# A two-layer decoder on one core: rotary turning by DMA exchange, paired causal tiles, 17-column values and second buffers in layer 1

## The chip, the cores and the metric

The kernel runs on one core of one Trainium2 chip. The metric is device time in microseconds (us) of one execution; the figure for a version is the median of its runs.

## The reference, cut to what matters

The model has two decoder layers over x of 4 sequences x 512 positions x 256 features (16 heads of 16), with a context of 1601 rows per sequence. The change lies in the self-attention of layer 1 and in what it shares with the cross-attention of layer 1:

```python
q = (x @ wq_w + wq_b).reshape(b, l, NH, HD)          # k and v in the same way
# apply_rope, for q and k: first and second are the halves (8 + 8) of a head
out = concatenate([first * cos - second * sin, second * cos + first * sin], -1)
scores = einsum('bnqh,bnkh->bnqk', q, k) / sqrt(HD)
scores = where(causal, scores, lowest)
attn = softmax(scores, axis=-1)
ctx = einsum('bnqk,bnkh->bnqh', attn, v)             # then @ wo_w + wo_b
```

Cross-attention of layer 1 has the same form without turning and mask, over the 1601 context rows. All of it is computed in float32.

## The kernel before, in words

The program has three parts, run one after the other: `front` (layer 0 attentions), `experts` (layer 0 feed-forward) and `heads` (all of layer 1). Only `heads` and the constants that it reads are changed.

`heads` takes the self-attention of all four sequences (`cross` False) and then the cross-attention of all four. A sequence has four groups of four heads (`head_group`, L1060). Two groups share one projection (`projections`, L1024) of 128 features on 128 partitions, called a half here, and one tile of values (`values`, L982).

A self-attention half goes this way. TensorE projects q into a PSUM bank, ScalarE (or VectorE) adds the bias into `q0` (L978). `rope` (L1012) then has TensorE multiply `q0` by a constant 128 x 128 matrix `rot`, which exchanges the halves of each head with a sign (L1014, through the helper at L239, "one<-q,consts" in the profile). VectorE multiplies that bank by the sines into `rt` (L1015), GpSimd multiplies `q0` by the cosines (L1017) and adds both into `qu` (L1019). k takes the same way into `ku`. `apart` (L1069) lets SyncE (SP) issue four DMAs for q and four for k in each group (L1072), which put each head's 16 rows at partition 32j of `qT` and `kT`, so that TensorE can hold four heads in four row lanes of 32.

A group then has two passes. In the first, 16 score units (one head, one block of 128 queries kq; 128, 256, 384 or 512 keys) each take a PSUM bank, "one<-kT,qT", and VectorE takes the largest masked score of each query (L1113). The negated maxima are turned by TensorE (L1147, "one<-consts,nm") and added to `qT`, giving `qa` (L1151), which frees the `qT` slot. In the second pass each of four key tiles t and four heads gives transposed scores, "one<-qa,kT", of 512, 384, 256 or 128 queries; ScalarE takes the exponential (L1173) into one of ten `pe` buffers, GpSimd zeroes the triangle (L1179), and TensorE multiplies four heads' weights by the values in four column lanes, "acc<-pe,v" (L1188). A head's values fill 32 columns: 16 values, a one (it gives the softmax's sum), 15 zeros. ScalarE copies the result (L243), TensorE turns it back (L1208), VectorE divides (L1212, L1220), and `finish` (L1281) projects and normalizes.

The order is made by `Plan` (L54) at build time: every step is a node with an engine, a cost and a priority; the plan keeps model clocks per engine, and issues in order of model start. TensorE nodes have a mode ("row" for four row lanes, "col" for column lanes, "full"), and the plan prefers to stay in one mode for a while. Pools of slots bound it: seven banks `one`, one bank `acc`, two slots of `qT`, `qa`, `v` and `q0`, three of `kT`, one of `rt`, `qu` and `ku`. On the chip each engine runs its list in this order and waits on semaphores[...].

Of the kernel before, what the change touches and what calls it, by code (L numbers as in the profile page):

```python
# [7 lines left out]
F32 = mybir.dt.float32  # L8
# [8 lines left out]
P = 128  # L17
# [12 lines left out]
NS = 31  # L30
NF = 24
# [5 lines left out]
C_ID, C_ROT, C_TRI, C_MQK = 0, 128, 256, 384  # L37
C_COS, C_SIN, C_IE, C_IT, C_IP = 896, 1408, 1920, 1936, 1968
NCONST = 1969
# [141 lines left out]
def cost_mm(n):  # L181

    return n * 4 / 2400
# [19 lines left out]
def tile_decoder(ctx: ExitStack, tc: tile.TileContext, a, out):  # L203
# [697 lines left out]
    def heads():  # L901
        plan = Plan()
        with tc.tile_pool(name="h1", bufs=1) as h1, \
# [5 lines left out]
            def slots(name, n, shape):  # L909
                plan.pool(name, n)  # L910
                return [h1.tile(shape, F32, tag=f"{name}{i}", name=f"{name}{i}") for i in range(n)]
# [4 lines left out]
            VV = slots("v", 2, [P, NKT, H // 2, 32])  # L916
# [9 lines left out]
            Q0, RT = slots("q0", 2, [P, L]), slots("rt", 1, [P, L])  # L926
            QU, KU = slots("qu", 1, [P, L]), slots("ku", 1, [P, LC])

            plan.pool("f", 6)
            FF = [*Q0, *RT, junk, *(h1.tile([P, L], F32, tag=f"f{i}", name=f"f{i}") for i in range(2))]  # L930
# [3 lines left out]
            rot = consts[:, C_ROT : C_ROT + P]  # L934
# [7 lines left out]
            def ones_behind(n, t):  # L942
                nc.gpsimd.memset(t[:, :, :, HD:], 0.0)
                nc.gpsimd.memset(t[:, :, :, HD : HD + 1], 1.0)

            def key_rows(n, k):
                nc.sync.dma_start(KT[k], a["keys0"])

            cleared = N("pool", 1.5, -1.5, clear)
            keyed = [N("dma", 2.5, -4.0, None, [N("sp", 0.4, -4.0, lambda n, k=k: key_rows(n, k))]) for k in range(3)]  # L950
            framed = [N("pool", 5.0, -1.5 + k, lambda n, k=k: ones_behind(n, VV[k])) for k in range(2)]


# [58 lines left out]
            def rope(pr, src, q0, rt, dst, DST):  # L1012

                r = N("pe", cost_mm(L), pr, lambda n: mm(ONE[n.slot], rot, Q0[q0.slot]), [src], take=["one"])  # L1014
                t = N("dve", dve(L), pr, lambda n: nc.vector.tensor_tensor(  # L1015
                    RT[rt.slot], ONE[r.slot], sinT, ALU.mult), [r], free=[r])
                d = N("pool", pool(L), pr, lambda n: nc.gpsimd.tensor_tensor(  # L1017
                    DST[dst.slot][:, :L], Q0[q0.slot], cosT, ALU.mult), [src], free=[q0])
                e = N("pool", pool(L), pr, lambda n: nc.gpsimd.tensor_tensor(  # L1019
                    DST[dst.slot][:, :L], DST[dst.slot][:, :L], RT[rt.slot], ALU.add), [d, t], free=[rt])  # L1020
                plan.frees(r, [q0])
                return e
# [37 lines left out]
            def head_group(cross, b, g, pos, vals, pair, after):  # L1060
# [8 lines left out]
                def apart(DST, dst, SRC, src, n):  # L1069
                    h0 = 64 * (g % 2)  # L1070
                    for j in range(4):
                        nc.sync.dma_start(DST[dst.slot][32 * j : 32 * j + HD, :n],  # L1072
                                          SRC[src.slot][h0 + HD * j : h0 + HD * (j + 1), :n])

                q, k = hold("qT", pr, after), hold("kT", pr, after)
                qd = N("sp", 1.6, pr, lambda n: apart(QT, q, QU, qu, L), [q, cleared, *qs])
                qready = N("dma", 0.5, pr, None, [qd], free=[qu])
                kd = N("sp", 1.6, pr, lambda n: apart(KT, k, KU, ku, nk), [k, *keyed, *ks])
# [6 lines left out]
                if cross:  # L1085
                    for n_ in range(12):
                        kq, m = divmod(n_, 3)
                        units += [(j, m, [(kq, m * 512, m * 512 + 512)]) for j in range(4)]
                else:
                    for kq in range(4):  # L1090
                        units += [(j, 0, [(kq, 0, (kq + 1) * P)]) for j in range(4)]
                maxes, scored = [], []
                for i, (j, m, prods) in enumerate(units):
                    pu = pos - 1.2 + (i + 0.5) / len(units)
                    js = slice(32 * j, 32 * j + 32)
                    nn, w = len(prods), prods[0][2] - prods[0][1]

                    def score(n, prods=prods, js=js, w=w):
                        for i, (kq, k0, k1) in enumerate(prods):
                            mm(ONE[n.slot][:, i * w : (i + 1) * w], QT[q.slot][js, kq * P : (kq + 1) * P],  # L1100
                               KT[k.slot][js, k0:k1])

                    s = N("pe", cost_mm(nn * w), pu, score, [mx], take=["one"], lanes=(j,), mode="row")

                    def largest(n, s=s, j=j, m=m, prods=prods, w=w):
                        nn, kq = len(prods), prods[0][0]
                        t = ONE[s.slot][:, : nn * w]
                        if cross:
                            nc.vector.tensor_reduce(  # L1109
                                MX[mx.slot][:, kq : kq + nn, j, m : m + 1], t.rearrange("p (a n) -> p a n", a=nn),  # L1110
                                AX.X, ALU.max)
                        else:
                            nc.vector.tensor_tensor_reduce(  # L1113
                                out=junk[:, :w], in0=t, in1=m_qk[:, 384 - kq * P : 512],
                                scale=1.0, scalar=NEG, op0=ALU.add, op1=ALU.max,
                                accum_out=MX[mx.slot][:, kq, j, 0:1])

                    maxes.append(N("dve", dve(nn * w), pu, largest, [s], free=[s]))
                    scored.append(s)
# [38 lines left out]
                for t in range(nkt):  # L1158
                    kn = kt_size(t) if cross else P
                    q0 = 0 if cross else t * P  # L1160
                    exps = []
                    for i, j in enumerate((2, 3, 0, 1)):
                        pu = pos + (t + 0.25 * i) / nkt
                        js = slice(32 * j, 32 * j + 32)
                        w = hold("pe", pu, [acc])

                        def score(n, t=t, kn=kn, q0=q0, js=js):
                            mm(ONE[n.slot][:kn, q0:], KT[k.slot][js, t * P : t * P + kn], QA[qa.slot][js, q0:])

                        s = N("pe", cost_mm(L - q0), pu, score, [w, o, *kready], take=["one"], lanes=(j,), mode="row")  # L1170

                        def weigh(n, s=s, w=w, kn=kn, q0=q0):
                            nc.scalar.activation(PE_[w.slot][:kn, q0:], ONE[s.slot][:kn, q0:], AF.Exp, scale=HD**-0.5)  # L1173

                        r = N("act", act(L - q0), pu, weigh, [s], free=[s])
                        if not cross:
                            def causal(n, w=w, q0=q0):
                                d = PE_[w.slot][:, q0 : q0 + P]
                                nc.gpsimd.affine_select(  # L1179
                                    d, d, pattern=[[1, P]], compare_op=ALU.is_ge, fill=0.0,  # L1180
                                    base=0, channel_multiplier=-1)

                            r = N("pool", pool(128), pu, causal, [r])
                        exps.append((w, r))

                    def product(n, t=t, kn=kn, q0=q0, exps=exps):
                        for j in range(4):
                            nc.tensor.matmul(  # L1188
                                ACC[acc.slot][32 * j : 32 * j + 32, q0:],
                                VV[v.slot][:kn, t, 4 * (g % 2) + j, :],  # L1190
                                PE_[exps[j ^ 2][0].slot][:kn, q0:],
                                start=t == 0, stop=t == nkt - 1,
                            )

                    pr_ = last[-1:] if last else []
                    last.append(N("pe", cost_mm(L - q0) + 0.05, pos + (t + 1.2) / nkt, product,
                                  [r for _, r in exps] + vready + pr_, free=[w for w, _ in exps], mode="col"))
# [220 lines left out]
def _constants():  # L1418
# [6 lines left out]
    for j in range(8):  # L1425
        for d in range(8):
            c[16 * j + d + 8, C_ROT + 16 * j + d] = -1.0
            c[16 * j + d, C_ROT + 16 * j + d + 8] = 1.0
# [4 lines left out]
    for d in range(P):  # L1433
        c[d, C_COS : C_COS + L] = np.cos(angle[d % 8])
        c[d, C_SIN : C_SIN + L] = np.sin(angle[d % 8])
# [6 lines left out]
def _layout(i):  # L1442
# [29 lines left out]
    o["w_shared_down"] = T(i["L0_ffn_w_down"])  # L1472
    for n in "qk":
        o[f"w{n}1"] = i[f"L1_attn_w{n}_w"]
        o[f"w{n}2"] = i[f"L1_xattn_W{n}"]
# [9 lines left out]
    cols = [i["L0_xattn_bq"], i["L0_xattn_bk"], i["L1_attn_wq_b"], i["L1_attn_wk_b"],  # L1485
# [29 lines left out]
```

## Time and profile before

| what | value |
|---|---|
| runs, us | 1762.3, 1764.39, 1764.44 |
| median of the runs | 1764.39 us |
| the profiled execution's own time | 1755.73 us |
| its span, first to last instruction | 1754.0 us |
| mean granted TensorE clock in it | 0.967 |
| first and last score unit of layer 1 ("one<-kT,qT") | 540.6 and 1677.8 us |
| last causal triangle (L1179) | 869.2 us |
| busy, 540 to 830 us | TensorE 280.7, VectorE 207.4, GpSimd 119.9, ScalarE 116.9 us |

A row of the groups names line, engine, operation, out<-in, and shapes; then count, busy time in us and mean ns of one. A float32 matmul shows as two records, so "x8" in the timeline is four heads of one matmul each. The timeline has start, duration and the records merged into the piece; a bracket gives the idle time ahead of it and what ended it. Matmul ends are modelled and overlap the next one's start, so lengths are taken from start to start. Self-attention and the first cross-attention group overlap between about 826 and 869 us.

### The profile page before, as it was taken

How to read it: one execution, taken by the hardware profiler on the slowest of the kernel's cores; microseconds unless marked ns; L12 is line 12 of the kernel's file. 1: busy time of each engine (PE TensorE's matmuls, PEld its weight loads, DVE VectorE, ACT ScalarE, POOL GpSimd, SP SyncE). 2: the span in 40 equal slices, each digit the busy share in tenths (PEclk: the TensorE clock that was granted, in tenths of full speed). 3: DMA queues.
4: the chain of work that ended last, by engine and by line, in shares of the span. 5: the costliest groups of instructions: out<-in, count | busy, mean ns of one | idle time of the engine just before them, and what ended most of it. 6: DMA issues, size and time to landing. Idle time of an engine off the chain costs nothing.

```text
span 1754.0 us, 28495 instructions
## 1 busy us (share of the span) xinstructions
PE 1661.4 (95%) x10756; PEld 862.5 (49%) x10756; DVE 1110.2 (63%) x2678; ACT 761.5 (43%) x1593; POOL 342.3 (20%) x521
## 2 busy tenths in 40 slices
PE   7899988999968999999999999999999999999995
PEld 4677775887754444454433334433334333343323
DVE  6997654121237766667776666777667776677625
ACT  0335551211112334444355555456554555545581
POOL 6652003432134534442100000100001000010000
PEclk9999987999988989999999999999999999999998
DMA  9000006876431100001100000001000010001000
GB/s 304 29 4 10 13 26 220 290 238 207 144 108 37 32 10 16 13 19 21 24 1 13 14 14 13 1 13 26 13 14 1 13 26 13 14 1 25 1 1 12
DMA packets 40843, 87.50 MB, mean 50 GB/s; under 512 B 7808, under 2 KB 26752, under 8 KB 37632
## 3 DMA queue, kind: packets, MB, share of 16 engines
q1 hardware_dynamic: 31728, 42.58, 9.0%
q0 software_dynamic: 8832, 43.00, 7.1%
q8 instruction: 86, 1.41, 0.3%
q14 instruction: 53, 0.43, 0.1%
q10 hardware_dynamic: 144, 0.07, 0.0%
HBM read 64.52 MB, written 8.26 MB: 41 GB/s over the span
## 4 chain that ended last, share of the span: by engine, by line
PE 83%; DVE 11%; DMA 2%; issue 2%; ACT 1%; POOL 1%; DVEq 0%; POOLq 0%; SPq 0%; ACTq 0%
PE one L239 53%; PE acc L1188 14%; PE e_one L239 11%; DVE junk L1113 1%; PE one L563 1%; PE one L1147 1%; PE one L1208 1%; DMA xs<-x_dram,tok 1%; PE one L1270 1%; DMA y<-ys_dram,dest 1%; DVE sc L423 1%; DVE pm L528 0%; ACT pe L1173 0%; DVE pr L462 0%; DVE qk L406 0%
## 5 line engine op out<-in xcount | busy, mean ns | idle before, releaser
L1173 ACT ACTIVATE pe<-one 128x512 f32<-128x512 f32 (+4 forms) x1088 | 533.0, 566 | 385.9 <-PE one L239 382.1
L1109 DVE TENSOR_REDUCE mx<-one 128x1 f32<-128x512 f32 x768 | 487.7, 683 | 182.1 <-PE one L239 178.3
L239 PE MATMUL one<-qa,kT 32*128 32x512 f32 (+4 forms) x2176 | 512.6, 600 | 7.7 <-ACT pe L1173 6.3
L239 PE MATMUL one<-kT,qT 32*128 32x512 f32 (+4 forms) x2560 | 500.7, 536 | 8.0 <-DVE mx L1113 2.6
L239 PEld LDWEIGHTS one<-qa,kT 32*128 32x128 f32 (+1 forms) x2176 | 171.8, 182 | 227.8 <-issue 78.0
L1188 PE MATMUL acc<-pe,v 128*32 128x512 f32 (+4 forms) x2176 | 270.7, 569 | 0.0
L239 PEld LDWEIGHTS one<-kT,qT 32*128 32x128 f32 x2560 | 191.5, 185 | 153.8 <-ACT pe L1173 45.3
L1276 POOL TENSOR_TENSOR x<-x,rows 128x1024 f32<-128x1024 f32 x12 | 28.3, 2356 | 802.4 <-PE one L1270 802.4
L1113 DVE CUSTOM_DVE_ANT_0 junk<-one,consts 128x256 f32<-128x256 f32 (+3 forms) x256 | 125.4, 490 | 50.7 <-PE one L239 25.8
L1188 PEld LDWEIGHTS acc<-pe,v 128*32 128x32 f32 (+1 forms) x2176 | 43.9, 108 | 178.6 <-issue 161.9
L1179 POOL TENSOR_SCALAR_AFFINE_SELECT pe<-pe 128x128 f32<-128x128 f32 x256 | 72.5, 298 | 140.9 <-ACT pe L1173 137.3
L239 PEld LDWEIGHTS e_one<-xsT,wgu 128*128 128x128 f32 x768 | 90.7, 194 | 4.8 <-issue 3.8
L239 PE MATMUL e_one<-xsT,wgu 128*128 128x128 f32 x768 | 90.6, 277 | 0.0
L239 PE MATMUL e_one<-xT,w_sgu 128*128 128x512 f32 x128 | 61.8, 624 | 3.1 <-DMA w_sgu<-in_w_shared_gu 3.1
L239 PE MATMUL one<-w_in,xT 128*128 128x512 f32 (+1 forms) x128 | 49.5, 543 | 10.4 <-DMA xT<-in_xT 10.4
L243 ACT COPY o<-acc 128x512 f32<-128x512 f32 x32 | 18.7, 586 | 75.5 <-PE acc L1188 75.5
L239 PE MATMUL one<-ctxT,q 128*128 128x512 f32 (+1 forms) x128 | 49.5, 518 | 0.0
L544 ACT ACTIVATE pe<-one,nm 128x512 f32<-128x512 f32 x64 | 37.3, 596 | 27.8 <-DVE nm L536 27.7
L239 PE MATMUL one<-pT,ctxN 128*128 128x128 f32 (+1 forms) x416 | 49.0, 275 | 0.0
L239 PEld LDWEIGHTS one<-pT,ctxN 128*128 128x128 f32 (+1 forms) x416 | 48.2, 192 | 1.6 <-issue 1.2
L852 DVE TENSOR_TENSOR he<-sg,e_one 128x512 f32<-128x512 f32 x24 | 16.5, 686 | 50.7 <-PE e_one L239 48.1
L830 DVE TENSOR_SCALAR xs<-xs,scs 128x256 f32<-128x256 f32 x24 | 8.5, 364 | 60.3 <-DMA xs<-x_dram,tok 60.3
(261 smaller groups left out, 1866.2 us busy)
## 6 DMA issues: line engine op xcount, KB each, us to landing
kT<-ku SPq DMA_DIRECT2D x64, 100.1 KB, 3.4
qT<-qu SPq DMA_DIRECT2D x128, 32.0 KB, 1.9
ctxN<-in_ctxN SPq DMA_DIRECT2D x4, 832.0 KB, 8.9
ctxT<-in_ctxT SPq DMA_DIRECT2D x4, 800.5 KB, 9.5
ys_dram<-ye SPq DMA_DIRECT2D x24, 128.0 KB, 2.4
kT<-in_keys SPq DMA_DIRECT2D x3, 800.5 KB, 9.7
xT<-in_xT SPq DMA_DIRECT2D x16, 128.0 KB, 3.6
x<-in_x SPq DMA_DIRECT2D x16, 128.0 KB, 6.0
```

The lines of the kernel that those rows point to most:

```text
L239: nc.tensor.matmul(out, lhsT, rhs, start=c == 0, stop=c == n - 1)
L243: nc.scalar.copy(dst, src)
L423: scores.append(N("dve", 1.21, pos + 0.22 + 0.05 * s, lambda n, s=s, pr=pr: nc.vector.tensor_reduce(SC[sc.slot][:, s].rearrange("p t h -> ...
L544: nc.scalar.activation(PE_[w.slot][:, : k1 - k0], ONE[b.slot][:, : k1 - k0], AF.Exp, bias=NM[nm.slot][:, 1:2], accum_out=PS[sm_.slot][:, i ...
L563: nc.tensor.transpose(ONE[n.slot][:kn, (t % 4) * P : (t % 4 + 1) * P], PE_[w.slot][:, (t % 4) * P : (t % 4) * P + kn], ident)
L1109: nc.vector.tensor_reduce(MX[mx.slot][:, kq : kq + nn, j, m : m + 1], t.rearrange("p (a n) -> p a n", a=nn), AX.X, ALU.max)
L1113: nc.vector.tensor_tensor_reduce(out=junk[:, :w], in0=t, in1=m_qk[:, 384 - kq * P : 512], scale=1.0, scalar=NEG, op0=ALU.add, op1=ALU.max, ...
L1147: nc.tensor.transpose(ONE[n.slot][:, kq * P : (kq + 1) * P], NM[nm.slot][:, kq].rearrange("p j r -> p (j r)"), ident)
L1173: nc.scalar.activation(PE_[w.slot][:kn, q0:], ONE[s.slot][:kn, q0:], AF.Exp, scale=HD**-0.5)
L1179: nc.gpsimd.affine_select(d, d, pattern=[[1, P]], compare_op=ALU.is_ge, fill=0.0, base=0, channel_multiplier=-1)
L1188: nc.tensor.matmul(ACC[acc.slot][32 * j : 32 * j + 32, q0:], VV[v.slot][:kn, t, 4 * (g % 2) + j, :], PE_[exps[j ^ 2][0].slot][:kn, q0:], s ...
L1276: rw = N("pool", pool(1024), pos, lambda n: nc.gpsimd.tensor_tensor(XB[b], XB[b], rows[:, row : row + D].unsqueeze(1).to_broadcast([P, 4, ...
```

## The change

1. Turning. The rows of wq and wk (and their biases) are laid out so that the 64 first halves of a half's eight heads lie on partitions 0 to 63 and the second halves on 64 to 127. `rope` no longer multiplies by `rot`: two DMAs exchange the two blocks of 64 partitions of `q0` into `rt`, and the multiplication by the (now signed) sines is given to VectorE or GpSimd. `apart` issues eight DMAs of 8 rows where it issued four of 16, for q and for k.
2. Pairs of masked tiles. The score units of the first pass are (kq 3), (kq 0 and 2), (kq 1), of 512, 128 + 384 and 256 columns; those of the second (t 0), (t 1 and 3), (t 2), of 512, 384 + 128 and 256. A pair shares one bank, and in the second pass one exponential. Maxima stay one instruction for each kq.
3. Values of 17 columns. The 15 zero columns go; `acc` is set to zero once at the start.
4. Second buffers for `rt`, `qu` and `ku`; the tree's pool `f` uses the second `rt` in place of one buffer of its own.

```diff
+MQ = (3,), (0, 2), (1,)
+TQ = (0,), (1, 3), (2,)
...
-            VV = slots("v", 2, [P, NKT, H // 2, 32])
+            VV = slots("v", 2, [P, NKT, H // 2, HD + 1])
...
-            Q0, RT = slots("q0", 2, [P, L]), slots("rt", 1, [P, L])
-            QU, KU = slots("qu", 1, [P, L]), slots("ku", 1, [P, LC])
+            Q0, RT = slots("q0", 2, [P, L]), slots("rt", 2, [P, L])
+            QU, KU = slots("qu", 2, [P, L]), slots("ku", 2, [P, LC])
...
-                r = N("pe", cost_mm(L), pr, lambda n: mm(ONE[n.slot], rot, Q0[q0.slot]), [src], take=["one"])
-                t = N("dve", dve(L), pr, lambda n: nc.vector.tensor_tensor(
-                    RT[rt.slot], ONE[r.slot], sinT, ALU.mult), [r], free=[r])
+                def swap(n):
+                    for i in range(2):
+                        nc.sync.dma_start(RT[rt.slot][64 * i : 64 * i + 64], Q0[q0.slot][64 - 64 * i : 128 - 64 * i])
+
+                r = N("dma", 0.7, pr, None, [N("sp", 0.8, pr, swap, [src])], free=[q0])
+                t = N("dve|pool", (dve(L) + 0.6, pool(L)), pr, lambda n: (nc.vector if n.on == "dve" else nc.gpsimd).tensor_tensor(
+                    RT[rt.slot], RT[rt.slot], sinT, ALU.mult), [r])
...
                     for j in range(4):
-                        nc.sync.dma_start(DST[dst.slot][32 * j : 32 * j + HD, :n],
-                                          SRC[src.slot][h0 + HD * j : h0 + HD * (j + 1), :n])
+                        for i in range(1 if cross else 2):
+                            w = HD if cross else HD // 2
+                            r = (h0 + j) * w + 64 * i
+                            nc.sync.dma_start(DST[dst.slot][32 * j + w * i : 32 * j + w * i + w, :n],
+                                              SRC[src.slot][r : r + w, :n])
...
-                qd = N("sp", 1.6, pr, lambda n: apart(QT, q, QU, qu, L), [q, cleared, *qs])
+                qd = N("sp", 1.6 if cross else 3.2, pr, lambda n: apart(QT, q, QU, qu, L), [q, cleared, *qs])
...
-                    for kq in range(4):
-                        units += [(j, 0, [(kq, 0, (kq + 1) * P)]) for j in range(4)]
+                    for kqs in MQ:
+                        units += [(j, 0, [(kq, 0, (kq + 1) * P) for kq in kqs]) for j in range(4)]
...
+                        def score(n, at=at, js=js):
+                            for t, kn, q0, w in at:
+                                mm(ONE[n.slot][:kn, w : w + L - q0], KT[k.slot][js, t * P : t * P + kn], QA[qa.slot][js, q0:])
+
+                        s = N("pe", cost_mm(w), pu, score, [e, o, *kready], take=["one"], lanes=(j,), mode="row")
+
+                        def weigh(n, s=s, e=e, kn=at[0][1], w=w):
+                            nc.scalar.activation(PE_[e.slot][:kn, :w], ONE[s.slot][:kn, :w], AF.Exp, scale=HD**-0.5)
...
-                                ACC[acc.slot][32 * j : 32 * j + 32, q0:],
+                                    ACC[acc.slot][32 * j : 32 * j + HD + 1, q0:],
```

## The prediction

> **What bounds the kernel now.** I read the page first: TensorE (PE) is busy for 95% of the span and carries 83% of the chain that ended last.
>
> ```profile
> PE 1661.4 (95%) x10756; PEld 862.5 (49%) x10756; DVE 1110.2 (63%) x2678; ACT 761.5 (43%) x1593; POOL 342.3 (20%) x521
> PE 83%; DVE 11%; DMA 2%; issue 2%; ACT 1%; POOL 1%; DVEq 0%; POOLq 0%; SPq 0%; ACTq 0%
> ```
>
> Then the busy times by stage (columns: PE, PEld, DVE, ACT, POOL busy, granted clock, DMA share, GB/s). In the self stage (540 to 830) PE is all but full, VectorE at 71%, the others at 40%; the cross stage is fuller still. So PE's own list is to be counted.
>
> ```profile
> 540.00:830.00 290.00, 280.67 (x1887) 140.09 (x1888) 207.35 (x742) 116.91 (x289) 119.92 (x274) 0.94 0.08 19
> 830.00:1700.00 870.00, 862.38 (x6022) 330.55 (x6020) 606.67 (x1175) 473.90 (x909) 33.77 (x77) 1.00 0.07 12
> ```
>
> What a piece of PE work costs I read from the timeline, start to start, at full clock:
>
> ```profile
> 705.27 1.06 PE L1188 MATMUL acc<-pe,v 128*32 128x512 f32 x8
> 706.26 0.71 PE L239 MATMUL one<-kT,qT 32*128 32x128 f32 x8
> 706.91 0.85 PE L1188 MATMUL acc<-pe,v 128*32 128x384 f32 x8
> 707.69 1.12 PE L239 MATMUL one<-q,consts 128*128 128x512 f32 x2
> 708.74 0.70 PE L239 MATMUL one<-qa,kT 32*128 32x256 f32 x8
> ```
>
> ```profile
> 1111.30 1.06 PE L1188 MATMUL acc<-pe,v 128*32 128x512 f32 x8
> 1112.29 1.14 PE L239 MATMUL one<-kT,qT 32*128 32x512 f32 x8
> 1113.37 1.06 PE L1188 MATMUL acc<-pe,v 128*32 128x512 f32 x8
> ```
>
> Column-lane products of 512 columns take 0.99, of 384 take 0.78: 0.21 for 128 columns (1.64 ns a column), hence 0.84 for 512 and **0.15 left over for each run in that mode**. A row run of 512 takes 1.08 (0.24 left over), one rotation 1.05 (0.21). A row run of four 128-column scores takes 0.65 for 0.21 of columns. So PE's time is columns of the fullest lane x 1.64 ns, plus 0.15 to 0.24 for each change of mode.
>
> **Removed from PE.** I counted both builds' instruction order in layer 1, taking for each run of one mode the lane with most columns. Rotations: 16 x 512 columns go, 16 x 0.84 = 13.4 us. Row lanes: 286,272 becomes 282,688 (the pairs come as four equal lanes more often), 3,584 x 1.64 ns = 5.9 us. Runs: row 404 to 378, full 184 to 165, col 267 to 253: 26 x 0.24 + 19 x 0.21 + 14 x 0.15 = 12.3 us. Together 31.6 us. Four of the rotations run between 525 and 558 us, where PE waits for norms and rotations anyway (busy 33 of 40 us from 520 to 560): 4 x 1.05 = 4.2 us that buy nothing. I take **27.4 us**, about 3.4 us of it in the cross stage (1,536 lane columns, 2.5 us, and five runs).
>
> **Off the path.** ScalarE: four exponentials of 600, 515, 403 and 288 ns become three of 600, 600 and 403, 0.2 x 64 = 13 us less on an engine at 40%; worth nothing while PE has other lanes to issue. VectorE: maxima unchanged (0.69 + 0.08 for 512 columns); 12 of 16 sine products of 0.69 leave it for GpSimd, which takes 12 x 1.27 = 15 us more (the row of the cosine product) and rises from 41 to some 51%. Both hidden by PE. One memset of `acc`, and 3 us less of memset on GpSimd, lie ahead of the first scores. The second `qu` and `ku` add nothing to PE; their worth is the earlier projections in the counted order.
>
> **Values of 17 columns.** No row shows 17. Weight loads take 109 ns for 32 columns and 184 for 128, 0.78 ns a column, so 15 columns fewer save 12 ns a load. If every load were exposed in its lane, 2176 x 12 ns / 4 = 6.5 us; if all are hidden, 0. A loss is not excluded by any row either, but a narrower copy writes the same 64 values per partition, and PE streams the same columns, so I bound it by 1 us. The loads mostly run beside matmuls: I take 0.
>
> **Added: waits on SP.** SP's list and landing times:
>
> ```profile
> 599.72 2.41 SPq L1072 DMA_DIRECT2D kT<-ku  x4
> 602.42 2.40 SPq L1072 DMA_DIRECT2D qT<-qu  x4
> ```
>
> ```profile
> qT<-qu SPq DMA_DIRECT2D x68, 32.0 KB, 1.9
> ```
>
> An issue costs 0.58 us (2.41 / 4 is 0.60), a landing 1.9. Now q needs eight: 8 x 0.58 + 1.9 = 6.5 us from `qa` (which frees the `qT` slot) to the last lane of the group after next, where it was 4.2. Each lane waits only for its own two DMAs, so lane 0 is ready after 3.1. Behind `qa` PE has in its list the 12 second-pass units of that group, a projection (1.9) and products (1.0), 5 us or more. The last lane can be late by 0 to 2 us in 14 groups, 0 to 28 us in all; most groups have cover, so I take 0.3 each, 4 us. SP's total is (256 + 64) x 0.58 = 186 us of some 265, and not a bound.
>
> **The exchange.** Bias to sine product was one matmul (1.05); now two issues and a landing, 1.2 + 1.9 = 3.1 us. 128 KB each could take longer: DMAs of 100 KB land in 3.5, so 3 to 5 us. SP issues the exchange of the next half behind eight q DMAs that wait for `qa`. If it is late, GpSimd stands in front of the sine product, and the triangles behind it on GpSimd hold the products on PE. The second `rt`, `qu` and `ku` let it start about a group (16 us) ahead. Between 0 and 2.5 us for each of six later halves: I take 2 us in all, near the low end since before, GpSimd held the weight loads of the products for 5.2 us in all this stage. At the start, q and k reach `qT` one exchange later, but two matmuls and VectorE's queue earlier: even. I take 0 of -4 to +4.
>
> The Trainium skill ("SBUF — State Buffer", its rule on the shared port pair) says that VectorE's two-input operation with both inputs in SBUF excludes a GpSimd operation that reads SBUF, for the whole instruction. The sine product was PSUM by SBUF, and becomes such a case. Row: GpSimd's cosine product is 1.27 us, VectorE's sine product 0.69. By the row alone nothing is added; by the rule four products left on VectorE block or are blocked once each, at most 4 x 1.3 = 5 us. No trace here shows a lock; I take 0 and keep 5 for the range.
>
> A second rule speaks against the change: "TensorE: Matmul & The Clock Gate", on the clock gate, has PE fall to half clock after some 3.4 us without work. This trace shows the price:
>
> ```profile
> 615.00 2.34 PE L239 MATMUL one<-kT,qT 32*128 32x512 f32 x4 [2.56 <-DVE mx L1113]
> ```
>
> ```profile
> 600.00:620.00 20.00, 17.44 (x110) 7.51 (x102) 15.78 (x55) 7.41 (x20) 12.82 (x23) 0.90 0.18 47
> 620.00:640.00 20.00, 20.00 (x130) 9.61 (x129) 10.45 (x40) 7.98 (x21) 8.85 (x19) 0.76 0.06 13
> ```
>
> One gap of 2.56 us and then a clock of 0.76 for 20 us and 0.90 before it: 2.6 + 4.8 + 2.0 = 9 us. By the row a gap below the rule's limit already costs that; by the rule gaps of 1 to 2 us would cost themselves only. My 6 us of new waits are many short ones, priced without the clock; with a gap of that kind each would be threefold.
>
> **Sum.** 27.4 - 4 - 2 = 21.4 us. The profiled execution (1755.7; span 1754.0 and 1.7 around it) would become 1734.3. The median of the runs stands 8.7 above the profiled one, so I forecast 1764.4 - 21.4 = **1743 us**.
>
> **Rivals.**
> (a) As summed, 1743, range 1730 to 1756 (new waits 0 to 17 us, values up to 6 us, start +-4): chance 0.56.
> (b) Larger gain. From 560 to 680 the clock of before was below full in four windows (0.91, 0.90, 0.76, 0.83: 1.8 + 2.0 + 4.8 + 3.4 = 12 us). If the fuller lanes and second buffers close the gaps that caused this, 27.4 + 12 = 39 us: 1725. For it: the gap at 612 waited for maxima behind a rotation, and rotations are gone. Against: gaps shift, they don't vanish, and the new ways are longer. Chance 0.17.
> (c) The waits eat the gain: q DMAs late by 1.4 us in 14 groups (20 us) and 1 us in six halves give 26 us: 1763, no change. For it: the plan prices eight issues at 3.2 us where they take 4.6. Against: it also prices PE at 0.85 for 512 columns where PE takes 1.08, so PE is behind the plan too. Chance 0.12.
> (d) Slower: the exchange stands behind q DMAs that wait for `qa`, GpSimd's triangles stand behind the sine product, PE's product behind these, for long enough to lower the clock. Price 9 us each as at 612; it decides from the third such gap (27 / 9). In six halves: 54 - 27 = +27, 1791. For it: three in-order lists in a row, SP, GpSimd, PE. Against: the exchange's lead of a group. Chance 0.15.
>
> A measurement of this kernel tells about 0.2% (3.5 us) from no change. Faster: (a), (b) and the better edge of (c), 0.75; within: 0.10; slower: (d), 0.15. The range reaches from (b) with the values' 6 us, 1719, to (c)'s far side, 1769; it leaves out most of (d).
>
> **What would show it.** No "one<-q,consts" matmuls; the stage from first score to last triangle (540.6 to 869.2, 329 us) shorter by about 20; the cross stage shorter by 3; 192 exponentials for 256 in self-attention; waits of "one<-kT,qT" on DMA and of the products on GpSimd below 10 us in all. Long GpSimd waits at the sine product with clocks below 0.9 beside them would mean (d). Wrong would be, too, a run overhead that is not removed with the run: the stage then shrinks by the rotations alone, some 10 us.

## The result, and the profile after

| | before | after |
|---|---|---|
| median of runs, us | 1763.88 (16 runs) | 1775.35 (16 runs, 1765.58 to 1782.16) |
| ratio, with 95% interval | | 1.0065 [1.0051, 1.008] |
| profiled execution; its span, us | 1755.73; 1754.0 | 1772.51; 1770.8 |
| mean granted clock in it | 0.967 | 0.953 |

The changed kernel is 0.65% slower, where 1743 us was forecast. (Ratios leave out runs more than 1.5% above the fastest of their kernel and medians do not, so the two can differ where a kernel's runs spread widely.)

The page of after, engine totals and the shares of the chain that ended last:

```profile
PE 1665.4 (94%) x10724; PEld 870.9 (49%) x10724; DVE 1095.6 (62%) x2659; ACT 762.2 (43%) x1537; POOL 351.5 (20%) x531
PE 80%; DVE 10%; DMA 3%; issue 2%; ACT 1%; SPq 1%; POOL 1%; DVEq 0%; POOLq 0%; ACTq 0%
```

The 32 records of the rotations are gone from PE (10756 before, 10724 after), yet PE's busy time is 4 us longer (1661.4 before): what is left ran slower. SPq, SyncE's issuing, is new in the chain with 1%. The stages of after:

```profile
540.00:830.00 290.00, 273.76 (x1829) 146.79 (x1831) 194.38 (x719) 111.11 (x229) 132.19 (x288) 0.89 0.15 32
830.00:1700.00 870.00, 863.15 (x5932) 329.99 (x5926) 604.26 (x1179) 465.31 (x884) 33.01 (x75) 0.98 0.07 13
```

In the self stage PE stood idle for 16.2 us (9.3 before) and the clock was 0.89 (0.94): 290 x 0.05 = 14.5 us more lost to the clock. The first cross-attention group lies in the second row; from 830 to 950 us the clock was 0.90 where it had been 1.00, 12 us more. From the first score to the last triangle after takes 337.1 us (542.8 to 879.9) where before took 328.6; 20 us less had been named as a sign of being right. The span behind the last triangle is 6.1 us longer. SP's timeline of after:

```profile
590.45 5.36 SPq L1079 DMA_DIRECT2D kT<-ku  x8
595.92 5.47 SPq L1079 DMA_DIRECT2D qT<-qu  x8
```

One issue in a run of eight takes 0.67 to 0.68 us (those in the runs of four of before took 0.60), so q and k of one group hold SP for 10.8 us where it was 4.8. What PE and GpSimd waited for (540 to 900 us for PE, to 880 for GpSimd; total, times, longest):

```profile
PE one L241 <- DVE mx L1120: 4.6, 7, 1.6
PE one L241 <- DMA kT<-ku: 3.4, 4, 2.7
```

```profile
POOL rt L1020 <- DMA rt<-q: 26.0, 5, 10.8
```

GpSimd did stand for 26 us in front of the sine product, as feared; but PE's waits for the q DMAs come to 0.5 us and the products' for triangles to 3.5. The waits on DMA and GpSimd together are 7.4 us, below the 10 that I had named as the sign of being right. So these waits alone do not make the loss; beside them stands a lower clock. PE's timeline has these small gaps (in brackets):

```profile
675.22 1.13 PE L241 MATMUL one<-kT,qT 32*128 32x512 f32 x2 [0.25 <-DMA kT<-ku]
676.56 2.04 PE L241 MATMUL one<-kT,qT 32*128 32x512 f32 x2 [0.21 <-DMA kT<-ku]
```

and these are 20-us windows of after:

```profile
660.00:680.00 20.00, 18.92 (x105) 9.35 (x108) 12.46 (x45) 8.62 (x19) 11.04 (x21) 0.90 0.11 19
700.00:720.00 20.00, 19.56 (x115) 10.19 (x115) 10.98 (x42) 6.66 (x14) 6.04 (x18) 0.74 0.17 34
740.00:760.00 20.00, 18.39 (x129) 10.02 (x129) 13.09 (x40) 6.80 (x15) 10.46 (x21) 0.83 0.14 27
```

The last two of these windows in before:

```profile
700.00:720.00 20.00, 19.93 (x162) 11.20 (x158) 12.44 (x43) 11.08 (x28) 9.82 (x25) 1.00 0.07 16
740.00:760.00 20.00, 19.78 (x157) 10.00 (x155) 13.13 (x51) 8.97 (x24) 9.56 (x25) 1.00 0.07 17
```

Read PE's busy time and the clock (third figure from the right) together: of the 20 us PE misses 0.4 to 1.6 in these rows of after, but the clock takes up to 5.2 (0.26 x 20). Before, PE waited 3.6 us for maxima and 1.1 for k between 540 and 900 us; both rows are longer after.

### The profile page after: what moved, and what is told of

Read it like the earlier page. It is cut to its first block, busy times and chain, and to the rows that moved or that the text cites. A ratio compares the mean times of both kernels' runs of the same rounds, so it can differ in the third digit from the quotient of the medians.

```text
span 1770.8 us, 28537 instructions
## 1 busy us (share of the span) xinstructions
PE 1665.4 (94%) x10724; PEld 870.9 (49%) x10724; DVE 1095.6 (62%) x2659; ACT 762.2 (43%) x1537; POOL 351.5 (20%) x531
## 4 chain that ended last, share of the span: by engine, by line
PE 80%; DVE 10%; DMA 3%; issue 2%; ACT 1%; SPq 1%; POOL 1%; DVEq 0%; POOLq 0%; ACTq 0%
PE one L241 52%; PE acc L1202 13%; PE e_one L241 10%; DVE junk L1120 2%; SPq L1079 1%; DMA xs<-x_dram,tok 1%; PE one L565 1%; PE one L1154 1%; PE one L1222 1%; PE one L1284 1%; ACT pe L1185 1%; DVE sc L425 1%; DVE pm L530 0%; DVE pr L464 0%; PE one L383 0%
## 5 line engine op out<-in xcount | busy, mean ns | idle before, releaser
L1185 ACT ACTIVATE pe<-one 128x512 f32<-128x512 f32 (+2 forms) x1024 | 526.8, 591 | 403.9 <-PE one L241 399.1
L241 PE MATMUL one<-qa,kT 32*128 32x512 f32 (+4 forms) x2176 | 519.9, 606 | 9.0 <-ACT pe L1185 6.8
L241 PE MATMUL one<-kT,qT 32*128 32x512 f32 (+4 forms) x2560 | 515.2, 546 | 8.3 <-DMA kT<-ku 3.4
L241 PEld LDWEIGHTS one<-qa,kT 32*128 32x128 f32 (+1 forms) x2176 | 180.5, 185 | 224.3 <-ACT pe L1185 69.3
L241 PEld LDWEIGHTS one<-kT,qT 32*128 32x128 f32 x2560 | 197.8, 191 | 167.0 <-issue 56.6
L1202 PE MATMUL acc<-pe,v 128*17 128x512 f32 (+4 forms) x2176 | 267.1, 568 | 0.0
L1202 PEld LDWEIGHTS acc<-pe,v 128*17 128x17 f32 (+1 forms) x2176 | 38.4, 96 | 179.3 <-issue 162.4
```

Source lines behind the costliest of these rows:

```text
L241: nc.tensor.matmul(out, lhsT, rhs, start=c == 0, stop=c == n - 1)
L1185: nc.scalar.activation(PE_[e.slot][:kn, :w], ONE[s.slot][:kn, :w], AF.Exp, scale=HD**-0.5)
L1202: nc.tensor.matmul(ACC[acc.slot][32 * j : 32 * j + HD + 1, q0:], VV[v.slot][:kn, t, 4 * (g % 2) + j, :], PE_[exps[j ^ 2][0].slot][:kn, w : ...
```

## The experiments

Theory C, formed on this: the doubled issues on SP make PE idle in short gaps, and the gaps lower the clock, which takes more than the gaps themselves. Its rivals: SP's load alone; the plan's wrong prices, that is, the order (later O); the exchange; the pairs (fuller lanes that hold banks longer, called V). W, in the expectations, is the exchange and the doubled issues taken together. All kernels follow in one table; the edits shown below it are shortened to their core. "Lost" is (1 - granted clock) x span, "rest" is span x clock, both means over the runs; PE is my count by the prediction's rule (columns of the fullest lane and modes; 1114.5 before, 1082.8 after).

| label | median us (runs) | ratio to before | clock | lost | rest | PE |
|---|---|---|---|---|---|---|
| before, all its runs beside these kernels | 1762.3 (145) | | 0.962 | 67.3 | 1693.2 | 1114.5 |
| after | 1775.35 (16) | 1.0065 [1.0051, 1.008] | 0.950 | 89.4 | 1684.2 | 1082.8 |
| e1_no_pairs | 1772.2 (20) | 1.0042 [1.0026, 1.0059] | 0.955 | 79.1 | 1691.5 | 1097.2 |
| e2_no_exchange | 1756.4 (20) | 0.9969 [0.9954, 0.9984] | 0.960 | 70.8 | 1684.4 | 1099.8 |
| e3_narrow_only | 1755.1 (4) | 0.9945 [0.9924, 0.9967] | 0.963 | 65.4 | 1688.9 | 1112.8 |
| e4_split_issues | 1779.8 (4) | 1.009 [1.0059, 1.0122] | 0.956 | 78.2 | 1699.6 | 1114.5 |
| e5_strided_four | 1755.8 (5) | 0.9957 [0.9929, 0.9985] | 0.956 | 76.8 | 1677.1 | 1082.8 |
| e6_strided_priced | 1760.1 (20) | 0.9979 [0.9964, 0.9994] | 0.952 | 83.8 | 1673.7 | 1079.4 |
| e7_true_prices | 1777.9 (4) | 1.008 [1.0054, 1.0106] | 0.943 | 100.8 | 1674.4 | 1077.7 |
| e8_cols17 | 1760.0 (15) | 0.998 [0.9967, 0.9993] | 0.961 | 68.0 | 1690.2 | 1114.5 |
| e9_idle_rotation | 1744.6 (4) | 0.9897 [0.9855, 0.994] | 0.968 | 55.4 | 1688.0 | 1097.9 |
| e10_gaps4 | 1778.5 (4) | 1.0091 [1.0066, 1.0115] | 0.959 | 73.3 | 1703.2 | 1123.9 |
| e11_gaps1 | 1778.9 (4) | 1.0089 [1.0065, 1.0113] | 0.959 | 73.3 | 1703.8 | 1123.9 |
| e12_strided_single | 1758.4 (20) | 0.997 [0.9956, 0.9985] | 0.956 | 76.5 | 1679.3 | 1097.2 |
| e13_order_alone | 1763.2 (4) | none | 0.955 | 80.0 | 1675.1 | 1081.9 |
| e14_idle_small | 1746.0 (10) | 0.9908 [0.9878, 0.9937] | 0.962 | 66.2 | 1679.5 | 1087.8 |
| e15_idle_again | 1754.9 (10) | 0.9948 [0.9923, 0.9972] | 0.963 | 65.4 | 1686.6 | 1097.9 |
| e16_changed_idle | 1758.5 (10) | 0.997 [0.9945, 0.9995] | 0.964 | 63.9 | 1691.4 | 1097.9 |
| e17_order_again | 1759.5 (12) | 0.995 [0.9916, 0.9984] | 0.954 | 80.4 | 1674.6 | 1081.9 |
| e18_small_again | 1743.1 (12) | 0.9934 [0.9903, 0.9965] | 0.963 | 64.6 | 1680.2 | 1087.8 |

**Doubled issues alone (e4).** Before, with eight DMAs of 8 rows for the four of 16; the plan's prices, and with them the order on PE, VectorE, ScalarE and GpSimd, stay those of before.

```diff
 for j in range(4):
-    dma_start(DST[32*j : 32*j + HD], SRC[h0 + HD*j : h0 + HD*(j + 1)])
+    for i in range(2):
+        r = h0 + HD*j + 8*i
+        dma_start(DST[32*j + 8*i : 32*j + 8*i + 8], SRC[r : r + 8])
```

> The kernel before, in the same order of instructions on every compute engine, with eight DMAs of 8 rows where it has four of 16 in self-attention, at unchanged plan costs. Theory W: 5 to 15 us slower than before (1769 to 1779 us), waits of the scores on kT and qT DMAs. Theory V: the same as before, 1762 to 1766 us.

Measured: +0.9%, some 16 us, with nothing else changed. In e4's trace PE's waits for k and q DMAs (540 to 900 us) are 9.1 us, where before had 1.1; over the runs rest is 6.4 us longer, and 11 us more are lost to the clock. More than half of the waiting, 5.4 us, stands at the first scores. SP's timeline and PE's:

```profile
530.00 11.34 SPq L1075 DMA_DIRECT2D qT<-qu  x16
541.45 11.49 SPq L1075 DMA_DIRECT2D kT<-ku  x16
```

```profile
544.24 0.71 PE L239 MATMUL one<-kT,qT 32*128 32x128 f32 x2 [3.65 <-DMA kT<-ku]
545.57 0.76 PE L239 MATMUL one<-kT,qT 32*128 32x128 f32 x2 [0.62 <-DMA kT<-ku]
546.91 0.76 PE L239 MATMUL one<-kT,qT 32*128 32x128 f32 x2 [0.58 <-DMA kT<-ku]
548.25 6.34 PE L239 MATMUL one<-kT,qT 32*128 32x128 f32 x26 [0.58 <-DMA kT<-ku]
```

The k DMAs stand behind sixteen q DMAs of two groups, and the lanes then start 1.33 to 1.34 us apart, which is two issues of 0.67: PE goes at the pace of SP. A later wait in e4's timeline, ahead of it one for ScalarE, and the 5-us windows around both:

```profile
767.54 0.88 PE L239 MATMUL one<-kT,qT 32*128 32x128 f32 x4 [0.53 <-ACT pe L1176]
769.37 0.56 PE L239 MATMUL one<-kT,qT 32*128 32x128 f32 x2 [0.94 <-DMA kT<-ku]
```

```profile
765.00:770.00 5.00, 3.53 (x19) 2.03 (x22) 1.38 (x7) 2.43 (x7) 2.13 (x8) 0.96 0.14 26
770.00:775.00 5.00, 5.00 (x33) 1.45 (x32) 1.86 (x10) 0.00 (x0) 0.00 (x0) 0.50 0.14 27
775.00:780.00 5.00, 5.00 (x28) 3.22 (x22) 2.32 (x9) 1.43 (x6) 1.59 (x6) 0.52 0.10 18
780.00:785.00 5.00, 4.58 (x27) 1.60 (x30) 4.35 (x13) 1.16 (x2) 1.27 (x1) 1.00 0.08 15
```

1.5 us of gaps, then ten microseconds at 0.50 to 0.52 with PE without a pause: 4.9 us lost behind them. That the gaps are the cause of the lower clock is theory C's claim; this row shows only that one follows the other.

**Halved issues in the changed kernel (e5).** The weights are laid out so that one head's 16 rows lie 8 partitions apart, and one strided DMA fetches them; order on the compute engines as in after.

```diff
-    for i in range(2): dma_start(DST[32*j + 8*i : ...], SRC[8*(h0 + j) + 64*i : ...])
+    dma_start(DST[32*j : 32*j + HD], SRC[h0 + j : 128 : 8])
```

> The changed kernel, instruction order untouched on TensorE, VectorE, ScalarE and GpSimd, with four DMAs instead of eight for a group's q or k: a head's 16 rows lie 8 partitions apart, so that one strided DMA takes both halves, and the exchange of blocks of 64 stays. If the doubled issues on SP are the cause (theory W in its narrow form): 1745 to 1757 us, as fast as the version with the rotation on TensorE or faster. If the exchange itself (its two DMAs, the landing, GpSimd's wait) is the cause: still 1768 us or more.

Measured: 19.6 us less than after, and faster than before; the exchange is still in it. SP's timeline of e5:

```profile
587.02 1.13 SPq L1017 DMA_DIRECT2D rt<-q  x2
588.25 2.45 SPq L1078 DMA_DIRECT2D kT<-ku  x4
```

Four again take 2.45 us. PE's waits for DMA do not appear in e5's list for 540 to 900 us. Of the 19.7 us by the means, rest gave 7.1 and the clock 12.6. So the doubled issues are the loss, shown from both sides: e4 has them without any exchange, e5 the exchange without them. (GpSimd's wait ahead of the sine product falls too, from 26.0 to 6.3 us; the exchange stands in the same list of SP.) The profiled executions side by side:

| | before | after | e4 | e5 |
|---|---|---|---|---|
| first score to last triangle, us | 328.6 | 337.1 | 344.5 | 315.1 |
| span behind the last triangle, us | 884.8 | 890.9 | 889.6 | 896.8 |
| PE's waits for k and q DMAs, 540 to 900 us | 1.1 | 3.9 | 9.1 | none |
| PE idle, 520 to 950 us | 15.9 | 22.2 | 22.2 | 14.6 |
| granted clock, 520 to 950 us | 0.95 | 0.89 | 0.90 | 0.91 |
| granted clock, 830 to 950 us | 1.00 | 0.90 | 0.93 | 0.87 |

e5 holds something that theory C does not foresee: its PE idles no more than before's and still has the lower clock, and of the 13.5 us that its stage is shorter, 12.0 come back behind it. A stretch of some 24 us at half clock begins there behind two gaps of 0.17 us; the gaps and 10 us of it:

```profile
847.27 0.43 PE L241 MATMUL one<-kT,qT 32*128 32x65 f32 x2 [0.17 <-DVE mx L1116]
847.87 1.72 PE L241 MATMUL one<-kT,qT 32*128 32x65 f32 x25 [0.17 <-DVE mx L1116]
```

```profile
850.00:855.00 5.00, 5.00 (x16) 1.71 (x14) 3.56 (x9) 0.77 (x2) 0.59 (x2) 0.50 0.17 21
855.00:860.00 5.00, 5.00 (x20) 1.71 (x19) 2.49 (x5) 0.59 (x1) 0.00 (x0) 0.50 0.44 71
```

**The plan's prices (e7, e6).** e7: after, with prices of 5.4 us for eight issues, 2.4 for four in cross-attention and 1.2 for the exchange; e6: e5 with 2.4 for every four and 1.2.

```diff
-N("sp", 0.8, pr, swap, [src])  ...  N("sp", 1.6 if cross else 3.2, ...)
+N("sp", 1.2, pr, swap, [src])  ...  N("sp", 2.4 if cross else 5.4, ...)   # e6: 2.4
```

> The changed kernel with its eight DMAs, and the plan told 5.4 us for eight issues and 1.2 for the exchange, against 3.2 and 0.8. If what hurts is that the order expects q and k too early: most of the loss comes back, 1750 to 1762 us. If it is the load on SP whatever the order: 1768 us or more.

> The same with the plan told what an issue takes (2.4 us for four, 1.2 for the exchange), so that the order changes. Counted TensorE time 1079 us against 1083 for the changed kernel and 1114 before. If issues are the cause and the order is right: 1740 to 1752 us. If order and prices matter little: as the run with the untouched order, within 3 us.

e7 was no better than after: had the order been at fault, most should have come back. e6 was not better than e5, though PE has 3.4 us less counted work in it; rest fell by 3.4 and lost rose by 7.

**Without pairs, without exchange, narrow alone (e1, e2, e3).** e1 has single units, e2 turns q and k by the matmul again and has four DMAs of 16 rows, e3 is both; e12 is e5 with single units.

```diff
-MQ = (3,), (0, 2), (1,)             # e1, e3, e12
+MQ = (0,), (1,), (2,), (3,)
-swap(): two DMAs                    # e2, e3
+mm(ONE[n.slot], rot, Q0[q0.slot])
```

> The changed kernel with single tiles instead of pairs (exchange by DMA, 17 columns and second buffers stay). Theory W (the exchange and the doubled DMA issues on SP make TensorE wait and lower its clock): no better than the changed kernel, 1770 to 1785 us. Theory V (a pair holds a bank for two maxima, so TensorE waits for banks behind VectorE): the gain of the removed rotations appears, 1745 to 1758 us.

> The changed kernel with the rotation back on TensorE and four DMAs of 16 rows (pairs, 17 columns and second buffers stay). Counted TensorE time is 15 us below the kernel before. Theory W: 1745 to 1755 us, clock 0.965 or more. Theory V: it stays slow, 1765 to 1778 us.

> Only 17 columns and the second buffers are left of the change. Both theories: the kernel before within 4 us (1760 to 1768 us); the values' narrower loads are worth 0 to 6 us at most. A third theory (the second buffers' new order is what hurts) would have it above 1770 us.

> The version with four strided DMAs without the pairs (counted TensorE time 1097 us against 1083). From the runs so far the pairs are worth nothing: 1752 to 1757 us. If TensorE's counted time sets the result: 1768 to 1771 us.

e1: without pairs 3 us faster than after, intervals overlapping; with four DMAs pairs are worth nothing either way (e2 against e3: 1.3 us slower with them; e5 against e12: 2.6 us faster). That settles V: it falls. Their 14.4 us of counted PE work appear nowhere in the time: in e5 against e12 lost and rest are alike within 2.2 us. e2, the exchange away and half the issues with it, has 1756.4, the same as e5 with the exchange, although e5 has 17.0 us less counted PE work: putting the exchange in the place of the rotations is worth about nothing. Whether the exchange costs what the rotations saved, or both are near nothing, e2 and e5 don't separate. e3, at 1755.1, is below the 1760 to 1768 that both theories expected of it.

**17 columns alone (e8).** Before, with values of 17 columns and the memset of `acc`.

```diff
-VV = slots("v", 2, [P, NKT, H // 2, 32])
+VV = slots("v", 2, [P, NKT, H // 2, HD + 1])
```

> The kernel before with values of 17 columns and the cleared accumulator only, no second buffers. If the 8.7 us of the narrow version come from shorter weight loads: 1753 to 1758 us. If they come from the second buffers' order: 1761 to 1765 us.

A gain of 0.2% [0.07, 0.33], some 2 to 4 us. The row of weight loads in after:

```profile
L1202 PEld LDWEIGHTS acc<-pe,v 128*17 128x17 f32 (+1 forms) x2176 | 38.4, 96 | 179.3 <-issue 162.4 <-ACT pe L1185 10.2 <-POOL pe L1192 3.5
```

96 ns a load, 108 before. With the second buffers (e3) the gain was 7 to 10 us, in another order of work, so that most of e3's gain goes with the buffers and their order.

**A price for a gap (e10, e11).** Before, with sixteen pauses planned in the cross stage: a small matmul that waits for four (e10) or one (e11) GpSimd memsets.

```diff
+w_ = N("pool", 0.0, pos + 0.4, pause, [last[5]])      # 4 or 1 memsets of gapt
+x_ = N("pe", 0.1, pos + 0.4, lambda n: mm(ONE[n.slot][:, :P], ident, gapt[:, :P]), [w_], take=["one"])
```

> The kernel before with 16 pauses in the otherwise gapless cross-attention: in each group one small matmul waits for four GpSimd memsets of 256 columns that start when a product ends (some 1.5 us), and the plan is not told. Theory C: each pause costs itself and 3.4 us or more of half clock after it: 60 to 100 us slower than before, clock near 0.93. If a gap costs only itself: 16 to 30 us slower.

> The same kernel, in the same order, with one memset in place of four (0.4 us; TensorE has about as much other work before it needs the result). Theory C with a threshold near 1 us: 3 to 15 us slower than before, of which 9 us are the added matmuls and changes of mode. If any short wait lowers the clock: 40 us or more.

Inconclusive. No idle time stood ahead of these matmuls in the traces, so the memsets had ended before PE came to them. Both cost 16 us: 9.4 us of counted PE work, and an order that moved. How much one gap costs by its length isn't shown by them.

**Work that nobody uses (e9, e16).** If gaps lower the clock, filling them should raise it. e9 is e5 with sixteen unused 512-column matmuls where the rotations stood, e15 the same kernel again; e16 is after with such matmuls.

```diff
+x_ = N("pe", cost_mm(L), pr, lambda n: mm(ONE[n.slot], ident, Q0[q0.slot]), [src], take=["one"], free=[q0])
```

> The version with four strided DMAs (1755.8 us) and, beside it, the 16 rotations back on TensorE as matmuls whose results nobody uses: 15 us more counted TensorE work. If TensorE's own work sets the time: 1767 to 1773 us. Theory C (what is taken off TensorE comes back as half clock after short idle gaps, so that its work is not the bound in this stage): 1751 to 1759 us, with a mean clock above 0.958.

> The version with 16 unused matmuls of 512 columns once more, beside the two others on one chip: 1740 to 1750 us.

> The changed kernel, with its eight DMAs for each q and k, and the 16 unused matmuls beside the exchange. Theory C with the SP path as the cause of the gaps: the filler bridges few of them, since they lie at the scores that wait for DMAs: 1762 to 1776 us, at most 10 us better than the changed kernel. If the filler alone sets the clock: 1745 to 1758 us.

With more work both were faster: after by 17 us (more than the at most 10 I expected), e5 by 11 in the four runs of e9 and by 1 in the ten of the same kernel as e15, which misses its 1740 to 1750. In e16 rest rose by 7 and lost fell by 25. But these matmuls also change the plan's order.

**Filler or order (e13, e17; e14, e18).** e13 and e17 keep e9's order and leave the matmuls out; e14 and e18 keep it with 128 columns.

```diff
-lambda n: mm(ONE[n.slot], ident, Q0[q0.slot])
+None                                                                  # e13, e17
+lambda n: mm(ONE[n.slot][:, :128], ident, Q0[q0.slot][:, :128])       # e14, e18
```

> The order of the version with 16 unused matmuls, with these left out (nothing else on TensorE is moved, the other engines' lists are the same). Theory C (the filler keeps TensorE's clock up): 1752 to 1760 us, clock 0.96 or less. If the order made the gain: 1735 to 1744 us.

> The same order with the 16 unused matmuls at 128 columns (some 0.3 us each) in place of 512 (1.05 us). Theory C: between the two, 1744 to 1755 us. If the order made the gain: 1737 to 1746 us.

> The kernel of e13 once more (the order of work that e9's plan gave, four strided DMAs, the unused matmuls left out), on the same chip as e18. If the order alone makes the gain of e14 (theory O), both medians are alike, near 1746 to 1753. If the unused matmuls themselves make it by filling the idle stretches of TensorE (theory C, half clock after short idle times), this one is 5 to 15 us longer than e18, 1757 to 1763, with a mean granted clock at least 0.008 lower.

> The kernel of e14 once more (the same order, with sixteen unused matmuls of 128 columns). Theory C: 1744 to 1750, granted clock about 0.963, and 5 to 15 us less than e17. Theory O: the same as e17 within 3 us.

e13 and e17 are one kernel, and so are e14 and e18, e9 and e15. On one chip e17 had a median of 1759.5 and e18 of 1743.1; the means differ by 10.2 us, with a 95% interval of 2 to 18 by resampling all twelve runs of each, but the ratios to before overlap (0.995 and 0.9934). With all runs of each kernel (16, 22 and 14) columns 0, 128 and 512 give lost 80, 65 and 63, rest 1675, 1680 and 1687. Without the unused matmuls the runs spread from 1736 to 1769 us, with those of 128 columns from 1737 to 1763. One and the same kernel differs in the clock: windows 540 to 830 us of the profiled executions of e14 (1759.1 us) and e18 (1740.1 us):

```profile
540.00:830.00 290.00, 283.68 (x1947) 156.84 (x1951) 204.09 (x743) 116.66 (x238) 130.99 (x288) 0.92 0.13 32
```

```profile
540.00:830.00 290.00, 282.35 (x1992) 156.08 (x1993) 212.38 (x758) 119.43 (x244) 132.52 (x292) 0.95 0.14 35
```

e13's profiled execution, without the matmuls and 1761.5 us long, has 0.91 there, hardly less than e14's 0.92. So no pair of traces shows the filler at work. That the small unused matmuls keep the clock up is likely by the runs, not settled. What the three kernels do show: 16 us more of counted PE work in one order of work (1081.9 to 1097.9) made none longer.

## Why the prediction was wrong

**The step that failed first** is "Added: waits on SP": "most groups have cover, so I take 0.3 each, 4 us". e4 and e5 measured 16 and 20 us for it. An issue took 0.67 in runs of eight, not 0.58. The added waiting of PE for these DMAs was 8 us in e4, twice my term and within its bounds of 0 to 28; but I had priced q behind `qa` only, while 8.2 of e4's 9.1 us are waits for k, and 4.4 of the 8 us arise at the first scores, where I had put the start at 0. The rest, 11 us, is clock. I had written "My 6 us of new waits are many short ones, priced without the clock", and chose the rule's view, that short gaps cost only themselves, over what a row of before hinted. The Trainium skill ("TensorE: Matmul & The Clock Gate", on the clock gate) asks for some 3.4 us without work; here 0.94 us was followed by 10 us at half clock. The measurement decides. SP's total was near the 186 us worked out (256 issues of 0.67 and the exchange's 32 at 0.58 are 190; the sum had 64 in the place of the 32), and no bound on average; the loss came where one group's issues stand behind another's.

**A second step failed: "Removed from PE".** Without the SP term the working gives a gain of 25 us (27.4 less 2 for the exchange). e5, which has no such waits, gains 7. My counts of columns and runs are right, and of the 31.6 us rest fell by 16 from before to e5 and by 20 to e6; but lost rose by 10 and 17. So at most two thirds was there as work, and much of that went to the clock. That the kernels with 0, 128 and 512 unused columns are not longer with more work says that PE's own list was not the bound that I took it for. Why a PE with less to do was granted less clock stays open; more idling is not the reason in e5's trace. Rotations against exchange, and pairs, both counted in full, were worth about nothing.

**The exchange**, 2 us: not measured by itself; e5 against e2 gives only the exchange less the rotations. One landed in 2.3 us in e5, below the 3 to 5 feared. **Values of 17 columns**, 0: the gain was 2 to 4 us, inside the bounds. **The second buffers** I had as adding nothing but their order; with them e3 gained some 5 us more than e8. **Shared ports**, 0: no run tried the sine products for themselves; what the traces show of a lock is below. **Off the path**: GpSimd rose by 12 us in the self stage (119.9 to 132.2), near the 15 less 3 that I had worked out, and the products' wait for triangles stayed at 3.5 us.

**Rivals.** (d) had the sign and the clock, but not the place: PE did not stand behind the triangles, and e4 loses as much without any exchange. Nor was its point of decision right: only one gap of after from 540 to 900 us (2.7 us, at the start) was of the 2.56-us kind; elsewhere half clock stood behind gaps of at most 1.6 us. (c) had the DMAs of SP, but q's and not k's, and counted only waits. (b) took the gap at 612 of before for one behind a rotation; in before's trace the maximum that ended it stood behind VectorE's small operations of a norm, one of which took 1.20 us.

**What stays open**: what decides whether a gap lowers the clock. Its length alone doesn't. Before had two gaps of 0.73 us at 904 and 908 us and stayed at 1.00; e4's 0.53 and 0.94 and e5's two of 0.17 stood ahead of half clock. After has one of the longest without any loss:

```profile
650.01 2.86 PE L241 MATMUL one<-kT,qT 32*128 32x256 f32 x22 [1.63 <-DVE mx L1120]
```

```profile
640.00:660.00 20.00, 18.37 (x137) 11.71 (x136) 12.49 (x51) 7.89 (x16) 6.15 (x16) 1.00 0.11 22
```

So it is shown that the doubled issues cost 16 to 20 us, and that more than half of this is clock; that PE's short gaps are what lowers the clock is argued from their order in time.

## What to carry to other kernels

Count the DMA issues of a queue before their bytes: doubling them on one busy in-order queue cost 16 us with the same bytes moved, and one strided DMA for each head gave it back. Look for the place where one group's issues stand behind another's, the start above all; the sum of the queue doesn't show it. Read busy time and granted clock together: a change that adds 8 us of short waits took 11 more in clock. Take a count of removed TensorE work as an upper bound: of 31.6 us counted, 7 arrived. Compare span x clock and span x (1 - clock) to see which of the two a change moved.

## What was not expected of the hardware

TensorE's clock fell to half behind gaps of 0.17 us (e5, 847 us) and of 0.53 and 0.94 us (e4, 767 us), and stayed full behind one of 1.63 us (after, 648 us). After with sixteen unused matmuls, and the order that the plan then makes, was 17 us faster (e16), and the fastest kernels found have such matmuls: e14 and e18, 1743 to 1746 us, 0.9908 [0.9878, 0.9937] and 0.9934 [0.9903, 0.9965]. A VectorE operation can be held by GpSimd: after's timeline has

```profile
739.86 1.27 POOL L1022 TENSOR_TENSOR qu<-q,consts 128x512 f32<-128x512 f32 x1 [9.91 <-ACT q L979]
739.98 1.17 DVE L1251 TENSOR_TENSOR lsd<-lsd 128x4 f32<-128x4 f32 x1
```

a VectorE operation of four columns takes 1.17 us, ending with GpSimd's, where the median of the 48 on this line is 0.16. The maxima behind it come a microsecond later, PE waits 1.47 us for one of them, and the window 740 to 760 has a clock of 0.83. Before's trace has three such operations too (1.20, 1.26 and 1.25 us at 611, 658 and 731 us), each beside the same cosine product of GpSimd; the prediction's "No trace here shows a lock" had missed them.
